# Two-layer graph network with neighbour quantiles: the kernel orders four queues by its own estimate of the engines

## The chip, the cores and the metric

The kernel runs on one core of one Trainium2 chip. The metric is the device time of one launch in microseconds (us); the time before is the median of three runs. The profile is one more execution, taken by the hardware profiler.

## The reference

There are 16 graphs of 1024 nodes with 64 features each (`x`: 16 x 1024 x 64, `adj`: 16 x 1024 x 1024 of zeros and ones, with self-loops). Two layers are computed, each followed by `layernorm(x + layer(x))`:

```python
# layer 0: thin out the neighbours, take quantiles, two dense layers
m = nb.sum(-1)                                   # neighbours without oneself
skip = where(m > 10, (m + 1) // 2, 1)
removed = nb & (skip > 1) & mask & ((rank + 1) % skip == 0)
valid = adj & ~(removed | removed.T)
sv = sort(where(valid, x[neighbour], big), over neighbours)   # for each node and feature
agg = sum over tau in (.25, .5, .75) of weight * interpolated sv[tau * (m - 1)]
y = relu((x + agg) @ W1 + b1) @ W2 + b2
# layer 1: messages of all neighbours
y = tanh(concat(x, adj @ x) @ W1 + b1) @ W2 + b2
```

The edge update of layer 1 doesn't reach the output and is left out.

## The kernel before

The work on a graph (a "batch" here) has three parts.

**Find** (`find`) loads the adjacency, turns it, ranks the neighbours on TensorE (`rank`), marks what is removed (VectorE, `removed`), adds up what stays (`stay`), and packs the neighbours of a node into words. The nodes of a batch are then sorted by their degree with a permutation matrix (`permutation`, `in_order`), and the numbers of each node's neighbours are drawn out with MAX8 and MATCH_REPLACE8, first from the words (`best_words`, `less_words`), then from codes made of them (`best_codes`, `less_codes`).

**Gather and sort.** 128 nodes of about equal degree are a tile; a batch has 8. Graphs go in groups: one batch, seven times two batches, one batch. `TILES` gives, for each tile of a group, the greatest and least count of cells. `gather` fetches, for the pair of tiles it is given, each neighbour's 64 features by one indirect DMA of GpSimd per cell (128 rows at a time; line L876), into one of a ring of four buffers g. `sort` then runs a sorting network over the cells: each step is one VectorE `tensor_tensor` min or max with two inputs, 64 to 1024 elements a partition. Only what the quantiles need is sorted. ScalarE multiplies the needed cells by their weights (L907), and TensorE adds them up (`add_up`, p_agg, L924 and L928). After that the ring's buffer is free.

**Close** (`close`) takes the sums back to node order (`back`, `return_to`), runs the dense layers, the norms, and layer 1, for which it loads the adjacency again and turns it in blocks.

The program is written as one stream. The comparisons of a pair of tiles go in a fixed merged order; find and close are lists of small steps (`Steps`), each with a weight in us, stretched over a time given beforehand, and a step is put between comparisons when its turn has come. "Time" is a counter `vector.now` in `Counted`, the wrapper through which all VectorE instructions are written (so they all stand at L443): it adds up the instructions' estimated durations. `Counted` also holds when GpSimd next wants to read its indices, `due`, every 1.32 us; if a comparison would come then, it writes first a `pause` (L437), a tiny one-input reduce of a cell written four comparisons ago. The framework then orders every engine's instructions itself, by its own model, within what the data allow.

Lists are made one group ahead while the present group is being gathered, and two ahead after that. A slot of the ring is given back a quarter into the next pair's comparisons. In the last group, `go_on_back` starts taking each pair back as soon as it is summed up.

Of the kernel before, what the change touches and what calls it, by code (L numbers as in the profile page):

```python
# [11 lines left out]
F32 = mybir.dt.float32  # L12
F16 = mybir.dt.float16
# [103 lines left out]
def network(n, least):  # L117
# [36 lines left out]
    return done, boxes(tuple((c, i) for i, c in enumerate(found))), found  # L154


@with_exitstack
def kernel(
# [236 lines left out]
    FINDING = 1.0  # L395
    CLOSING, CLOSING_LAST = 0.8, 60.0
    TURNING = 40.0
    RING = 4
    GATHER = 1.32
    pause = const.tile([P, 1], F32, name="pause")  # L400

# [6 lines left out]
    class Counted:  # L408

# [3 lines left out]
        def __init__(self):  # L413
            self.now = 0.0
            self.due = 0.0
            self.written = []

        def __getattr__(self, name):
            def size_of(x):
                n = 1  # L420
                for step, size in x.ap[1:]:
                    n *= size
                return n

            def issue(out, *args, **more):
                inputs = [a for a in args if isinstance(a, bass.AP)]
                n = max([size_of(out)] + [size_of(a) for a in inputs])
                each, more_us = 0.00104, 0.0
                if name in ("tensor_scalar", "tensor_copy"):
                    each = 0.00032 if out.dtype in (BF16, F16) and inputs[0].dtype in (BF16, F16) else 0.00053  # L430
                if name == "match_replace" or "accum_out" in more:
                    more_us = 0.07
                us = 0.067 + more_us + n * each
                two = name in ("tensor_tensor", "tensor_add", "tensor_sub", "tensor_mul",
                               "scalar_tensor_tensor")
                if two and self.now >= self.due and len(self.written) >= 4:
                    nc.vector.tensor_reduce(pause, self.written[-4], AX.X, ALU.max)  # L437
                    self.due = self.now + GATHER
                    self.now += 0.065
                elif not two and self.now + us >= self.due:  # L440
                    self.due = max(self.now, self.due) + GATHER
                self.now += us
# [3 lines left out]
    vector = Counted()  # L446

    class Steps:
# [3 lines left out]
        def __init__(self, within):  # L452
            self.steps, self.at, self.within = [], 0, within
            self.due = vector.now
# [13 lines left out]

        def go(self, all_of_it=False):
            scale = self.within / sum(us for us, _, _ in self.steps)  # L470
            while self.at < len(self.steps) and (all_of_it or self.due <= vector.now):
                us, what, args = self.steps[self.at]
                what(*args)
                self.at, self.due = self.at + 1, self.due + us * scale
# [5 lines left out]
    class Group:  # L480


        def __init__(self, number, start, G):
# [4 lines left out]
            self.pairs = [(k, k + 1) for k in range(0, NT * G, 2)]  # L488
# [6 lines left out]
    def find(group, i, within, pools):  # L495
# [7 lines left out]
        def begin():  # L503
            v["x_s"] = lists.tile([P, NT, C], F32, name="x_f", bufs=1)
            nc.sync.dma_start(v["x_s"], x[b].rearrange("(t p) c -> p t c", p=P))
            v["nb"] = mats.tile([P, NT, N], BF16, name="nb", tag="mat")
            v["a"] = [mats.tile([P, HT, N], F32, name="a", tag="mat") for _ in range(2)]
            for t in range(0, NT, 2):
                nc.sync.dma_start(v["a"][t // HT][:, t % HT:t % HT + 2],
                                  adj[b, t * P:(t + 2) * P, :].rearrange("(t p) k -> p t k", p=P))  # L510

        def adjacent(t):
# [3 lines left out]
            else:  # L516
                nc.scalar.activation(v["nb"][:, t], v["a"][t // HT][:, t % HT], AF.Sign)  # L517
# [8 lines left out]
        def features(i):  # L526
            if i == 0:
                v["part"] = lists.tile([P, NT, C], F32, name="part", bufs=1)
                nc.scalar.copy(part_of[0], v["x_s"])
            elif i == 1:  # L530
                vector.tensor_sub(v["part"], v["x_s"], part_of[0])
            elif i == 2:
                nc.scalar.copy(part_of[1], v["part"])
# [8 lines left out]
        def turn(j):  # L542
            p = ps.tile([P, NT, P], BF16, name="p_nb", tag="f")
            for t in range(NT):
                nc.tensor.transpose(p[:, t], v["nb"][:, t, block(j)], ident_h)  # L545
            if alone and j % 2:
                vector.tensor_scalar(v["nb_t"][:, j], p.rearrange("p t c -> p (t c)"), 0.0, None, op0=ALU.max)
            else:
                nc.scalar.activation(v["nb_t"][:, j], p.rearrange("p t c -> p (t c)"), AF.Relu)  # L549

        for k in range(4):
            to.add(1.5, features, k)
# [5 lines left out]
        def by_block(h):  # L558
# [4 lines left out]
            for j in range(NT):  # L563
                nc.tensor.matmul(v["p_cnt"][:NT, half], in_block[:, j], v["nb_t"][:, j, half],  # L564
                                 start=(j == 0), stop=(j == NT - 1), skip_group_check=True)
            nc.scalar.copy(v["blocks"][:, half], v["p_cnt"][:NT, half])
# [904 lines left out]
```

## Time and profile before

| what | value |
|---|---|
| median of three runs | 3017.12 us (3016.63 to 3021.24) |
| profiled execution | 3815.42 us, span 3813.7 us |
| mean granted TensorE clock, profiled | 0.709 |
| VectorE busy, profiled | 2329.5 us, 9225 instructions |
| GpSimd busy, profiled | 2104.7 us, 1943 instructions, 1859 of them gathers into g |
| first and last gather start | 103.7 us, 3683.2 us |

The profiled execution took 798 us more than the median of the runs. Its durations of single instructions can be used; its waits are those of that execution. In a row of the profile, `g<-in_x_dram,index` says what is written from what, `x1859 | 2075.7, 1117` is the count, the busy us and the mean ns of one, and behind it stands the time the engine was idle just before, and what ended most of it. All of VectorE's instructions stand at L443 (pauses at L437), so they are told apart by their tiles.

### The profile page before, as it was taken

What the parts mean: (1) busy time and instruction counts of PE and PEld (TensorE: products, weight loads), DVE (VectorE), ACT (ScalarE), POOL (GpSimd) and SP (SyncE); (2) the same over time, 40 slices, a digit from 0 to 9 for tenths busy, and PEclk for the clock granted to TensorE, in tenths of its full rate; (3) what the DMA queues carried; (4) which work ended last, traced back from release to release, by engine and by line L of the source; (5) the groups of instructions that cost most, each with busy time, mean ns of one, the idle gap of its engine ahead of it and who ended that gap; (6) DMA issues with size and microseconds to landing.
All of it is one profiled execution on the core that took longest, in us unless ns stands there. A gap on an engine that the chain in (4) does not pass through costs nothing.

```text
span 3813.7 us, 37663 instructions
## 1 busy us (share of the span) xinstructions
PE 1942.5 (51%) x10312; PEld 1070.0 (28%) x10312; DVE 2329.5 (61%) x9225; ACT 1324.3 (35%) x2945; POOL 2104.7 (55%) x1943
## 2 busy tenths in 40 slices
PE   5206523731565442963439635674336645674376
PEld 3103312420333221532224323332113323242133
DVE  4208624991598635885268844877248765768653
ACT  3204423431443332542325323544224334134123
POOL 1760346077654766167572677447571576757750
PEclk9556756765788666875669756786667866777578
DMA  2101111121212201222022212032021321242111
GB/s 99 20 19 48 58 50 32 65 52 24 64 44 87 66 18 62 82 66 43 17 67 93 67 30 65 23 105 64 18 66 28 94 58 26 60 117 62 20 47 29
DMA packets 268306, 205.67 MB, mean 54 GB/s; under 512 B 92634, under 2 KB 225290, under 8 KB 268086
## 3 DMA queue, kind: packets, MB, share of 16 engines
q1 hardware_dynamic: 207382, 147.10, 12.1%
q0 software_dynamic: 59744, 55.90, 7.5%
q8 instruction: 83, 1.36, 0.2%
q14 instruction: 137, 1.12, 0.1%
q10 hardware_dynamic: 960, 0.18, 0.0%
HBM read 203.97 MB, written 4.19 MB: 55 GB/s over the span
## 4 chain that ended last, share of the span: by engine, by line
PE 30%; another core or an unknown queue 25%; DVE 22%; ACT 9%; issue 8%; POOL 4%; DMA 1%; SPq 0%; ACTq 0%; DVEq 0%; POOLq 0%
DVE g L443 12%; PE p_msg L1144 5%; POOL g L876 4%; PE p_srt L687 3%; PE p_g L965 3%; PE p_adj L1135 2%; PE p_rank L596 2%; PE p_rank L593 2%; PE p_agg L924 2%; PE p_cnt L564 1%; PE p_nb L545 1%; ACT nb_t L549 1%; ACT g L907 1%; DVE codes L443 1%
## 5 line engine op out<-in xcount | busy, mean ns | idle before, releaser
L876 POOL DMA_INDIRECT g<-in_x_dram,index x1859 | 2075.7, 1117 | 1470.3 <-issue 560.1
L443 DVE TENSOR_TENSOR g<-g 128x128 f32<-128x128 f32 (+7 forms) x4982 | 1581.3, 373 | 199.7 <-remote 93.7
L545 PE MATMUL p_nb<-ident_h,nb 128*128 128x128 bf16 x1024 | 107.9, 280 | 649.6 <-DVE nb L443 261.9
L437 DVE TENSOR_REDUCE pause<-g 128x1 f32<-128x2 f32 x1021 | 148.5, 145 | 272.2 <-ACT g L907 240.5
L907 ACT ACTIVATE g<-g,weights 128x64 f32<-128x64 f32 x1006 | 260.0, 338 | 102.7 <-DVE g L443 84.3
L965 PE MATMUL p_g<-back,parts 128*64 128x512 bf16 x720 | 197.9, 425 | 186.6 <-DVE back L443 138.5
L443 DVE TENSOR_SCALAR gone<-gone,s 128x1024 bf16<-128x1024 f16 x128 | 64.3, 503 | 362.8 <-ACT gone L598 222.8
L598 ACT ACTIVATE gone<-p_rank,s 128x1024 f16<-128x1024 f32 x128 | 141.5, 1112 | 402.2 <-remote 303.2
L545 PEld LDWEIGHTS <-nb 128*128 128x128 bf16 x1024 | 92.6, 130 | 670.4 <-issue 489.9
L1144 PE MATMUL p_msg<-adj_t,x 128*64 128x512 f32 x416 | 232.3, 661 | 65.9 <-issue 30.4
L593 PE MATMUL p_rank<-after,blocks 8*128 8x512 bf16 x256 | 121.4, 474 | 282.0 <-ACT gone L598 147.5
L549 ACT ACTIVATE nb_t<-p_nb 128x1024 bf16<-128x1024 bf16 x124 | 122.1, 1023 | 375.0 <-remote 247.9
L924 PE MATMUL p_agg<-g,ident 128*128 128x128 f32 x918 | 161.6, 332 | 131.3 <-ACT g L907 83.7
L687 PE MATMUL p_srt<-pay,perm 128*128 128x323 bf16 x1024 | 187.0, 320 | 52.0 <-DVE x_q L443 29.4
L625 ACT ACTIVATE valid<-p_stay 128x1024 bf16<-128x1024 f32 x128 | 130.4, 1019 | 173.5 <-remote 95.0
L924 PEld LDWEIGHTS p_agg<-g,ident 128*128 128x128 f32 x918 | 143.0, 236 | 151.9 <-ACT g L907 96.4
L1137 ACT COPY adj_t<-p_adj 128x512 f32<-128x512 f32 x208 | 117.4, 584 | 162.6 <-PE p_adj L1135 79.0
L596 PEld LDWEIGHTS <-nb_t 128*128 128x128 bf16 x1024 | 70.6, 111 | 365.1 <-issue 365.1
L618 PE MATMUL p_stay<-nb,ident_h 128*128 128x512 bf16 x256 | 115.1, 450 | 105.8 <-ACT valid L625 56.3
L965 PEld LDWEIGHTS <-parts 128*64 128x64 bf16 x720 | 80.0, 119 | 280.1 <-issue 178.8
L517 ACT ACTIVATE nb<-a 128x1024 bf16<-128x1024 f32 x124 | 125.4, 1051 | 67.2 <-remote 27.1
L1135 PE MATMUL p_adj<-ident,a_block 128*128 128x128 f32 x832 | 138.6, 300 | 14.3 <-ACT z_t L1156 11.6
(188 smaller groups left out, 3054.9 us busy)
## 6 DMA issues: line engine op xcount, KB each, us to landing
a<-in_adj_dram SPq DMA_DIRECT2D x64, 1024.0 KB
a_block<-in_adj_dram SPq DMA_DIRECT2D x208, 256.0 KB
g<-in_x_dram,index POOLq DMA_INDIRECT x1859
a_ahead<-in_adj_dram SPq DMA_DIRECT2D x48, 256.0 KB
x_f<-in_x_dram SPq DMA_DIRECT2D x16, 256.0 KB
out_dram<-o SPq DMA_DIRECT2D x16, 256.0 KB
x_c<-in_x_dram SPq DMA_DIRECT2D x15, 256.0 KB
few<-index SPq DMA_DIRECT2D x45, 0.0 KB
```

The costliest lines, as they stand in the source:

```text
L437: nc.vector.tensor_reduce(pause, self.written[-4], AX.X, ALU.max)
L443: return getattr(nc.vector, name)(out, *args, **more)
L545: nc.tensor.transpose(p[:, t], v["nb"][:, t, block(j)], ident_h)
L549: nc.scalar.activation(v["nb_t"][:, j], p.rearrange("p t c -> p (t c)"), AF.Relu)
L593: nc.tensor.matmul(p[:, half_of(h)], v["blocks"][:, block(t)], after[:, half_of(h)], start=True, stop=False, skip_group_check=True)
L687: nc.tensor.matmul(p[:, k, :PAY], v["perm"][:, t, block(2 * at + k)], pay[:, t], start=(t == 0), stop=False, skip_group_check=True)
L876: nc.gpsimd.indirect_dma_start(out=part[:, j, :], out_offset=None, in_=x_rows, in_offset=bass.IndirectOffsetOnAxis(ap=group.index[:, v, sl ...
L907: nc.scalar.mul(g[:, cell], g[:, cell], group.weights[:, v, u, place:place + 1])
L924: nc.tensor.matmul(p, ident, it, start=(k == 0), stop=(k == most - 1), skip_group_check=True)
L965: nc.tensor.matmul(v["p_g"][h][:C, :HALF], v["parts"][:, k, q], m[:, half_of(h)], start=(k == 0 and v["start"]), stop=(k == 2 and q == v[" ...
L1135: nc.tensor.transpose(p[:, block(t)], m[:, t], ident)
L1144: nc.tensor.matmul(v["p_msg"][C:2 * C, :HALF], v["x1"][:, j, :], adj_t, start=(j == 0), stop=(j == NT - 1))
```

## The change

All `nc.tensor`, `nc.scalar`, `nc.sync` calls in the steps go through wrappers that estimate when an instruction can start and end. Inside the main loop, VectorE, TensorE, ScalarE and SyncE keep the order in which the program is written; GpSimd is left to the framework. The next comparison of a pair is picked among those whose inputs are ready, by how it fits GpSimd's next reading. When the reading is due, one of the one-input steps of find or close is put there if it is about due, else a pause, which now reads a constant. When an instruction's inputs are estimated to be late, comparisons are put in front of it. Tile k is paired with the tile k from the end. Lists are made up to two groups ahead at all times, and paced by when the gathers would run dry. Some rests and lags between steps are longer, and some buffers more.

```diff
+def order_of(n, least):            # which comparison must wait for which
...
-    FINDING = 1.0
-    CLOSING, CLOSING_LAST = 0.8, 60.0
+    IN_ORDER = {DVE, PE, Activation, SP}
+    FINDING_FIRST, FINDING = 95.0, 105.0
+    CLOSING, CLOSING_LAST = 110.0, 60.0
+    SPARE, EACH, EARLY, PACE, AHEAD, LATE = 10.0, 1.4, 3.0, (0.45, 1.2), 1.0, 2.0
+    ALONE = ("best_words", "less_words", "best_codes", "less_codes", "permutation", "removed", "back")
...
-    class Counted:
+    class Machine:                 # now, due, gathered; when each part of a tile was made and used
+        def ready(self, reads, writes):
+        def note(self, reads, writes, end):
...
+    class Engine:
+        def takes(self, name, out, reads):
+            n = max(size_of(a) for a in [out] + reads)
+            if self.kind == "ACT":
+                return 0.057 + 0.000845 * n, 0.12
+            if self.kind == "SP":
+                return 0.06, 2.0 + size_of(out) * out.ap[0][1] * 4e-6 / 0.2
+            if name == "transpose":
+                return (0.22 if reads[0].dtype == F32 else 0.107), 0.16
+            n = size_of(out)
+            return (max(0.43, 0.00168 * n) if reads[0].dtype == F32 else max(0.056, 0.00042 * n)), 0.16
...
+                if ready > machine.now + AHEAD:
+                    machine.fill(ready - AHEAD)
...
+    class Vector:
...
+                if ready > m.now:
+                    m.fill(ready)
+                    m.now = max(m.now, ready)
...
-                if two and self.now >= self.due and len(self.written) >= 4:
-                    nc.vector.tensor_reduce(pause, self.written[-4], AX.X, ALU.max)
+        def pause(self):
+            if machine.now >= machine.due:
+                nc.vector.tensor_reduce(pause, fill[:, :2], AX.X, ALU.max)
+                machine.due = machine.now + GATHER
+                machine.now += 0.065
...
     class Steps:
+        def pace(self):
+            left = sum(us for us, _, _ in self.steps[self.at:])
+            if self.until is None:
+                return self.within / sum(us for us, _, _ in self.steps)
+            return min(max((self.until() - machine.now) / max(left, 1.0), PACE[0]), PACE[1])
+        def alone(self, early):    # does the next step if it is one of ALONE and due within `early`
...
-            self.pairs = [(k, k + 1) for k in range(0, NT * G, 2)]
+            self.pairs = [(k, NT * G - 1 - k) for k in range(NT * G // 2)]
...
-        to.lagged(NT, (2.5, rank, 0), (0.1, removed, 3))
+        to.lagged(NT, (2.5, rank, 0), (0.1, removed, 5))
...
-                group.x_q[i] = lists.tile([P, NT, C], F32, name="x_q", bufs=4)
+                group.x_q[i] = lists.tile([P, NT, C], F32, name="x_q", bufs=6)
...
-                group.index = lists.tile([P, G, LIST], I32, name="index")
+                group.index = lists.tile([P, G, LIST], I32, name="index", bufs=3)
...
     def gather(group, at, sorts, lists):
...
             if start > filled[at % RING]:
-                least = 1
+                copy(part, none[:, :, None].to_broadcast([P, 2 * n, C]))
...
+            ready = machine.ready([group.index], [part])
+            machine.gathered = max(machine.gathered, machine.now, ready) + (many - 1) * EACH
+            landed.append(machine.gathered + 2.0)
...
-            for there, here, j in few(G):
-                nc.sync.dma_start(parts[0][here, j], got[there])
+            def give():
+                for there, here, j in few(G):
+                    nc.sync.dma_start(parts[0][here, j], got[there])
+            later.append((machine.gathered + 3.0, give))
...
+    def choose(tiles, latest):
+        gap = machine.due - machine.now
+        few, found = [], None
+        for t in tiles:
+            for n in t.ready[:5]:
+                wait = 0.05 if t is latest and t.last is not None and n in t.after[t.last] else 0.0
+                few.append((wait + 0.1 * (1 - t.left / t.all), t.us[n] + wait, t, n))
+        few.sort(key=lambda c: c[0])
+        if sum(us for _, us, _, _ in few) > gap > 0:
+            for some in range(1, 1 << len(few)):
+                these = [c for k, c in enumerate(few) if some >> k & 1]
+                over = sum(us for _, us, _, _ in these) - gap
+                if over >= 0:
+                    cost = over + sum(c[0] for c in these) / len(these)
+                    if found is None or cost < found[0]:
+                        found = cost, these[0]
+            return found[1][2:]
+        return few[0][2:]
...
+        def dry():
+            return machine.gathered + EACH * sum(TILES[g.G][k][0] - 1 for g, at in to_gather
+                                                 if g.number in found for k in g.pairs[at]) - SPARE
...
+            def turn(self):        # class Sorting
+                tiles = [t for t in self.tiles if t.ready and t.landed <= machine.now]
+                if not tiles:
+                    return False
+                if machine.now >= machine.due:
+                    if not any(steps.alone(EARLY) for steps in [f[2] for f in finding] + closing):
+                        vector.pause()
...
+                self.latest, n = choose(tiles, self.latest)
+                self.latest.issue(n)
...
-            ahead = 1 if to_gather and to_gather[0][0].number <= now else 2
-            if not finding and to_find and to_find[0][0].number <= now + ahead:
+            if not finding and to_find and to_find[0][0].number <= now + 2:
...
+                    steps.until = lambda group=group, i=i: min(begun + FINDING, dry() if i == group.G - 1
+                                                               else begun + (dry() - begun) / 2)
...
+        with tc.manual_schedule(engines=IN_ORDER):
+            for group in groups:
...
+                    sorting = Sorting(tiles, (group, at))
+                    machine.fill = sorting.fill
+                    while not sorting.done:
+                        around(group.number)
+                        if not sorting.turn():
+                            machine.now += 0.1
```

## The prediction

> **What bounds the kernel now.** I read the page's busy rows first, then the row of the gather, then who GpSimd (POOL) waited for, then the order of time in one quiet and one crowded stretch.
>
> ```profile
> PE 1942.5 (51%) x10312; PEld 1070.0 (28%) x10312; DVE 2329.5 (61%) x9225; ACT 1324.3 (35%) x2945; POOL 2104.7 (55%) x1943
> PE 30%; another core or an unknown queue 25%; DVE 22%; ACT 9%; issue 8%; POOL 4%; DMA 1%; SPq 0%; ACTq 0%; DVEq 0%; POOLq 0%
> L876 POOL DMA_INDIRECT g<-in_x_dram,index x1859 | 2075.7, 1117 | 1470.3 <-issue 560.1
> L443 DVE TENSOR_TENSOR g<-g 128x128 f32<-128x128 f32 (+7 forms) x4982 | 1581.3, 373 | 199.7 <-remote 93.7
> L437 DVE TENSOR_REDUCE pause<-g 128x1 f32<-128x2 f32 x1021 | 148.5, 145 | 272.2 <-ACT g L907 240.5
> ```
>
> No engine is full here, but the profiled execution (span 3813.7 us, 3815.42 us in all) is 798 us longer than the median of the three runs, 3017.12 us. A quarter of its chain is "another core or an unknown queue": mostly ScalarE waiting for a result of TensorE whose semaphore comes 10 to 27 us after the last matmul shown, while gathers run. All of PE, ACT and DVE stand still together for 634 us, and 509 us of that ends at such a late semaphore (added up from the trace). The runs without a profile have no room for it, so I take it as a thing of this execution and rebuild the runs' time from GpSimd's queue, which has to do 1867 gathers one by one.
>
> The quiet stretch and the crowded one (order of time; start, duration, engine, line):
>
> ```profile
> 158.56 0.99 POOL L876 DMA_INDIRECT g<-in_x_dram,index  x1 [0.30 <-issue]
> 159.86 0.99 POOL L876 DMA_INDIRECT g<-in_x_dram,index  x1 [0.30 <-issue]
> ...
> 3446.36 0.89 DVE L443 TENSOR_TENSOR g<-g 128x256 f32<-128x256 f32 x3
> 3446.42 1.23 POOL L876 DMA_INDIRECT g<-in_x_dram,index  x1 [0.30 <-issue]
> ...
> 3447.17 0.15 DVE L437 TENSOR_REDUCE pause<-g 128x1 f32<-128x2 f32 x1
> 3447.23 1.42 DVE L443 TENSOR_TENSOR g<-g 128x256 f32<-128x256 f32 x4
> 3447.95 1.58 POOL L876 DMA_INDIRECT g<-in_x_dram,index  x1 [0.30 <-issue]
> ...
> 3448.64 1.65 DVE L443 TENSOR_TENSOR g<-g 128x384 f32<-128x384 f32 x4
> 3449.83 1.01 POOL L876 DMA_INDIRECT g<-in_x_dram,index  x1 [0.30 <-issue]
> ```
>
> Alone, a gather starts every 1.30 us (0.99 + 0.30). Beside comparisons one takes 1.23 or 1.58 us and the next starts 1.53 and 1.88 us later. Over all 1842 successive pairs of gathers the step from start to start is 1.32 us where comparisons cover under 5% of it (771 pairs) and 1.56 us where they cover over 30% (911 pairs); its median is 1.41 us where they cover over 60%, so a tail makes the mean. Gathers delayed by over 0.3 us are 217 and hold 162 of the 226 us of delay.
>
> ```profile
> POOL g L876 <- PE p_agg L928: 331.4, 7, 101.1
> POOL g L876 <- ACT g L907: 156.9, 2, 156.6
> POOL g L876 <- PE p_agg L924: 126.2, 7, 33.7
> POOL g L876 <- DVE mid L443: 84.3, 1, 84.3
> ```
>
> These and smaller ones are the 900 us in which GpSimd had no gather to start: a list not made yet, or a ring slot not given back. So the profiled span is 103.7 (first gather) + 1842 x 1.44 = 2652 + 900 in gaps with some 27 of the gathers around them + 130 after the last gather.
>
> For the median run I keep everything but the gaps. With the same comparisons in less time, the crowded share rises from 911/1842 = 49% by 59/44 (the 1581 us of comparisons over about 2700 us, against over 3580) to 66%, so the mean step is 0.66 x 1.56 + 0.34 x 1.32 = 1.478 us. That gives 104 + 1867 x 1.478 = 2759 + 130 = 2993, and 24 us of gaps are left to make 3017. **The runs are bound by GpSimd's gathers, and mainly by what a comparison on VectorE costs each of them.**
>
> **The change, part by part.**
>
> *Comparisons by GpSimd's next reading* (`choose`, `pause`). Now two tiles' steps are merged by a fixed rule, and a step of up to 1.2 us can begin just before GpSimd wants to read. The change picks, among up to ten ready comparisons, those whose sum ends at the reading, so the overshoot falls from about half a step (mean 0.317 us) to near nothing. Bounds for a crowded gather: 1.32 us (never in the way) and 1.56 us (as now; worse is possible if the estimate drifts). I take 1.41, today's median in the crowded case: the tail is what a choice can take away. A thinner total raises the crowded share to 70%: 0.7 x 1.41 + 0.3 x 1.32 = 1.383, x 1867 = 2582, a gain of 177 us on 2759.
>
> *One-input steps in place of a pause* (`alone`). A pause is followed by the next comparison 0.06 us later, so 1021 cost about 65 us of VectorE, which is not the bound: 0 us. But of the 88 such steps of a batch (20 + 12 of words, 20 + 12 of codes, 8 each of permutation, removed, back), 24 are 16-bit `tensor_scalar` ones. Here a rule speaks against the change. Row: a gather that has such a permutation beside its reading steps 1.54 us in the median (15 of them), one with MAX8 on the words 1.30 us (19 of them). The Trainium skill, "SBUF — State Buffer", section "Who interferes with whom", says that `tensor_scalar` in a two-port mode holds the pair shared with GpSimd for the whole instruction and locks the other out, and that one-input work outside those modes doesn't. By the rule the 24 x 15 = 360 steps would cost their whole 0.48 us each, 173 us, and the gain would vanish; by the row 0.24 us, 86 us if all were put at a reading. Today's clock also counts them as openings, so I book nothing more and keep 86 us for the range.
>
> *Lists further ahead, their own paces, more buffers* (`now + 2` always, `dry`, `x_q` 6, `index` and `weights` 3). Worth at most the 24 us of gaps left. At the start of the second group the wait stays: 130 gathers last 180 us and two lists must be made in 2 x 95 us. I book 50 us of gaps against 24, since the order is now fixed. Lower bound 10, upper in the rival.
>
> *Pairs balanced.* Gathers and comparisons by pair (0.067 + 1.04 ns an element a step, the code's own rate, beside 0.283 us measured for 128 elements with overlap) go from 54 gathers with 50.1 us and 18 with 10.9 us to 42 with 38.7 us and about 28 with 18 to 22 us. The ring's slots come free evenly: inside the gaps. In the last group the last pair is (3, 4) instead of (6, 7), 18.9 us of comparisons for 12.9; most lies under its own gathers. The last tile alone is 9.3 for 6.2 us: +4 us on the tail, 134.
>
> *Order by hand on four queues.* It adds no instruction and no DMA. SP's small transfers into g (`few`) move behind an estimate, so that SP is not blocked by them; the summing after the last gather stays outside the hand order. What it costs is waiting at the head of a queue: at zero while VectorE has slack. VectorE is busy 2329.5 us, 52.7 of it before the first gather and 62.8 after the last, so 2214 us in a gather stretch of 2632: 418 us of slack, 28 us for each of the 15 later batches. That is the cover; the first rival takes it away.
>
> *Start.* Zeroing whole ring tiles on GpSimd is about 20,700 elements a partition at the trace's 0.98 us for 960, some 21 us from 11 us on, done before 104 us; SP, too, loads as before. 0 us.
>
> Sum: 104 + 2582 + 50 + 134 = **2870 us**, 147 below 3017 (4.9%).
>
> **The rivals.**
>
> *Slower: VectorE stands behind the list and close steps.* With a fixed order a `removed`, `x_q` or `d` that waits for TensorE holds every comparison behind it. For it: the estimate takes TensorE at full clock, while the page shows half and 0.709 in the mean; one `rank` runs 2.13 us on TensorE in the trace (126.69 to 128.82 us) against 0.88 in the estimate. VectorE's waits for such results (gone 362, s 102, x_q 93, d 82, low 39 us) are about 680 us now, 42 us a batch. 15 x 42 = 630 less 418 of slack is 212: 2870 + 212 = 3082 us. It decides from 28 us a batch, and 3017 is passed at 38. Against it: those waits are swollen by this execution's late semaphores, and `removed` now lags `rank` by five steps.
>
> *The step doesn't shrink.* The choice works blind: if VectorE or GpSimd runs off the estimate, comparisons still meet readings, and the 16-bit steps add theirs. Then 104 + 2759 + 134 + 10 = 3007 us, between 2985 and 3025: the change would not do what it says.
>
> *Better still.* Crowded gathers at 1.34 us, gaps 10: 104 + 1867 x 1.34 + 134 + 10 = 2750 us.
>
> **How the numbers follow.** About 0.2%, 6 us, is what a measurement can tell from no change. Chances: the forecast 0.52 (own range 2810 to 2940), better still 0.08, the step doesn't shrink 0.14 (0.09 of it faster, 0.03 the same, 0.02 slower), the slower rival 0.26 with one in a hundred of it the same. Faster 0.69, same 0.04, slower 0.27. The range runs from 2760, near the better case, to 3085, which takes in the slower rival's own figure; the worse half of that rival, about 0.13, and some 0.05 below stay out.
>
> **What would show it.** Right: gathers beside comparisons step 1.38 to 1.44 us and few exceed 1.3 us in duration; fewer `pause` rows than 1021 by several hundred; GpSimd's waits for `p_agg` and for list results shrink; still 1859 gathers. Wrong: VectorE's rows waiting for ACT or PE results grow past 28 us a batch with GpSimd waiting for `p_agg` (slots late) behind them; or gathers beside permutation, removed and back at 1.5 us and over, with the mean step unchanged. A first gather later than 110 us or a tail over 145 us would each take their difference off the gain. If TensorE's late semaphores stay in the profile, its span can go either way, and only the timed runs count.

## The result, and the profile after

The changed kernel takes **3038.93 us** (median of 4 runs, 3036.05 to 3041.53), the kernel before 3019.18 us (4 runs): a ratio of 1.0065, 95% interval 1.0048 to 1.0082. It is 0.65% slower, where 4.9% less was forecast. The profiled execution took 3041.53 us (span 3039.8, granted clock 0.766), so this profile can be read as the time itself. That of before could not, but times like its 3815 us are met without the profiler too: on three chips used below, timed runs of before took 3862, 3936 and 3902 us in the median, at a granted clock of about 0.70, and such runs ("late results" below) are compared only among themselves.

The page of the changed kernel, in the same rows as before: the busy line, the chain by engine, and the three groups.

```profile
PE 1904.4 (63%) x10326; PEld 1060.5 (35%) x10326; DVE 2403.2 (79%) x9330; ACT 1322.1 (43%) x2946; POOL 2084.7 (69%) x1951
PE 4%; DVE 3%; DMA 1%; ACT 1%; issue 0%; SPq 0%; DVEq 0%; ACTq 0%
L1042 POOL DMA_INDIRECT g<-in_x_dram,index x1859 | 2045.9, 1101 | 822.5 <-issue 525.5
L1088 DVE TENSOR_TENSOR g<-g 128x128 f32<-128x128 f32 (+6 forms) x4982 | 1588.3, 373 | 122.7 <-DMA g<-few_x 109.5
L579 DVE TENSOR_REDUCE pause<-fill 128x1 f32<-128x2 f32 x1125 | 163.5, 145 | 0.0
```

The chain says little here: it was followed back for 9% of the span only, so what bounds the kernel has to be read from queues. The same 1859 gathers are busy 30 us less than in the profile of before. VectorE has 1125 pauses for 1021, and it is busy for 79% of the span.

From the trace, start to start, 1854 gathers follow one another without a gap at 1.405 us in the mean: 1.435 where comparisons and other two-input work cover over 30% of the step (1312 of them, 71%), 1.312 where they cover under 5%. The span is then 114.9 (first gather) + 2605 + 189 (176 of gaps, and the 12 gathers beside them) + 131.0 (tail) = 3040 us. The waits of GpSimd that make up the gaps:

```profile
POOL g L1042 <- issue: 525.5, 1699, 8.1
POOL g L1042 <- DVE index L574: 106.8, 5, 66.5
...
POOL g L1042 <- DVE g L1088: 25.8, 8, 14.5
POOL g L1042 <- PE p_agg L539: 21.5, 3, 12.5
POOL g L1042 <- ACT g L539: 17.4, 5, 8.6
```

"issue" is mostly the 0.30 us between any two gathers. Of the 176 us of gaps, 107 are a list that isn't made yet (index: 66.5 us once, at 298 us, then 40 us in four waits at later group changes, the longest 16.0), and 69 are slots of the ring that come back late (p_agg and g, and one under "issue"; seven waits).

Who is late can be seen in VectorE's own waits. First the waits of the changed kernel's VectorE between first and last gather; the columns are us in total, times, and the longest:

```profile
DVE gone L574 <- ACT gone L539: 137.3, 63, 4.6
DVE g L1088 <- DMA g<-few_x: 109.5, 8, 22.4
DVE part L574 <- ACT pay L539: 39.7, 11, 19.9
DVE ln_st L574 <- ACT ln_st L539: 29.7, 17, 4.7
```

Added up, these and the smaller ones are 482 us of waits for results of ScalarE, TensorE and the small transfers. For a gather VectorE waits 2 us in the whole run. The table of windows (before, between, and behind the gathers; us, busy us and instructions of PE, PEld, DVE, ACT, POOL, then granted clock, DMA share and GB/s) has VectorE busy 2282 of 2794 us between them:

```profile
0.00:114.90 114.90, 57.44 (x369) 30.96 (x369) 60.85 (x230) 32.66 (x44) 30.76 (x85) 0.86 0.23 80
114.90:2908.80 2793.90, 1749.48 (x9576) 978.14 (x9577) 2282.30 (x8910) 1245.39 (x2814) 2052.48 (x1866) 0.76 0.26 68
2908.80:4500.00 1591.20, 97.50 (x384) 51.36 (x382) 60.04 (x193) 44.00 (x88) 1.51 (x1) 0.98 0.01 4
```

2282 + 482 = 2764 of 2794 us. That such a sum fills the stretch says little by itself, since an engine is nearly always busy or waiting; what tells is whom it waits for. **VectorE never gets ahead of the gathers any more, and the work that makes the lists and frees the slots passes through its queue.** The experiments show how much of the gaps this explains, and how much it doesn't. One group change (order of time on VectorE, then on GpSimd):

```profile
2021.74 0.67 DVE L574 TENSOR_REDUCE ln_st<-ln_sq 128x8 f32<-128x512 f32 x1
2027.08 0.20 DVE L574 RECIPROCAL ln_st<-ln_st 128x8 f32<-128x8 f32 x1 [4.67 <-ACT ln_st L539]
2027.20 0.51 DVE L574 TENSOR_REDUCE x_q<-p_srt 128x128 f32<-128x384 f32 x1
2027.62 0.68 DVE L574 TENSOR_TENSOR o<-d,ln_st 128x512 f32<-128x512 f32 x1
2028.22 0.55 DVE L574 TENSOR_REDUCE x_q<-p_srt 128x128 f32<-128x384 f32 x1
2032.55 0.56 DVE L574 TENSOR_REDUCE x_q<-p_srt 128x128 f32<-128x384 f32 x1 [3.78 <-ACT srt L539]
```
```profile
2038.62 1.00 POOL L1042 DMA_INDIRECT g<-in_x_dram,index  x1 [0.31 <-issue]
2055.62 0.99 POOL L1042 DMA_INDIRECT g<-in_x_dram,index  x1 [16.00 <-DVE index L574]
```

A close's `ln_st` waits 4.67 us for ScalarE at the head of the queue; the list's `x_q`, which stands behind it, starts by as much later, and a later `x_q` then waits itself. The plan wanted the list 10 us before the gathers ran out; it is there 16 us after. These two waits are 8.4 us of that; the rest had come together before.

### The profile page after: what moved, and what is told of

It reads as the page before. It is cut to its first block, busy times and chain, and to the rows that moved or that the text cites. A ratio compares the mean times of both kernels' runs of the same rounds, so it can differ in the third digit from the quotient of the medians.

```text
span 3039.8 us, 37578 instructions
## 1 busy us (share of the span) xinstructions
PE 1904.4 (63%) x10326; PEld 1060.5 (35%) x10326; DVE 2403.2 (79%) x9330; ACT 1322.1 (43%) x2946; POOL 2084.7 (69%) x1951
## 5 line engine op out<-in xcount | busy, mean ns | idle before, releaser
L1042 POOL DMA_INDIRECT g<-in_x_dram,index x1859 | 2045.9, 1101 | 822.5 <-issue 525.5
L1088 DVE TENSOR_TENSOR g<-g 128x128 f32<-128x128 f32 (+6 forms) x4982 | 1588.3, 373 | 122.7 <-DMA g<-few_x 109.5
L539 PE MATMUL p_agg<-g,ident 128*128 128x128 f32 (+1 forms) x1108 | 185.0, 338 | 162.7 <-ACT g L539 162.7
L539 PEld LDWEIGHTS p_agg<-g,ident 128*128 128x128 f32 x1108 | 177.2, 251 | 177.8 <-ACT g L539 153.2
L539 PE MATMUL p_nb<-ident_h,nb 128*128 128x128 bf16 x1024 | 93.2, 252 | 229.3 <-DVE nb L574 154.4
L539 PE MATMUL p_adj<-ident,a_block 128*128 128x128 f32 x832 | 152.9, 315 | 25.7 <-DMA a_block<-in_adj_dram 18.6
L539 PEld LDWEIGHTS <-nb 128*128 128x128 bf16 x1024 | 78.3, 115 | 254.9 <-issue 244.8
L579 DVE TENSOR_REDUCE pause<-fill 128x1 f32<-128x2 f32 x1125 | 163.5, 145 | 0.0
L539 PEld LDWEIGHTS p_adj<-ident,a_block 128*128 128x128 f32 x832 | 105.0, 160 | 148.7 <-issue 136.2
L539 PEld LDWEIGHTS <-perm 128*128 128x128 bf16 x1024 | 96.8, 103 | 106.4 <-DVE perm L574 31.3
```

Source lines behind the costliest of these rows:

```text
L539: return getattr(self.engine, name)(out, *args, **more)
L579: nc.vector.tensor_reduce(pause, fill[:, :2], AX.X, ALU.max)
L1042: nc.gpsimd.indirect_dma_start(out=part[:, j, :], out_offset=None, in_=x_rows, in_offset=bass.IndirectOffsetOnAxis(ap=group.index[:, v, sl ...
L1088: nc.vector.tensor_tensor(out, *ins, op=op)
```

## The experiments

Times are medians; each ratio is to before on the same chip, with its 95% interval. "Step", "gaps" and "tail" are worked out from each trace as above. For e1 to e4, for e5 to e12 (without e10) and for g15 before took 3018.66, 3017.83 and 3016.41 us: TensorE's results came in time.

| kernel | us | ratio | step us | gaps us | tail us |
|---|---|---|---|---|---|
| changed | 3038.93 | 1.0065 | 1.405 | 176 | 131.0 |
| e1: before, pause on a constant | 3076.66 | 1.0193 | 1.516 | 21 | 98.5 |
| e2: first lists in 60 us | 3044.15 | 1.0075 | 1.402 | 172 | 131.3 |
| e3: no order by hand | 3153.96 | 1.0444 | 1.506 | 103 | 107.0 |
| e4: no choice | 3036.05 | 1.0052 | 1.435 | 122 | 118.5 |
| e5: always a pause | 3020.93 | 0.9999 | 1.402 | 175 | 123.2 |
| e6: no 16-bit steps for a pause | 3018.68 | 1.0002 | 1.407 | 159 | 125.4 |
| e9: next batch's first steps early | 3029.06 | 1.0047 | 1.400 | 169 | 129.3 |
| e12: TensorE estimated slower | 3302.71 | 1.0954 | 1.393 | 469 | 115.5 |
| g15: five edits together | 3077.70 | 1.0204 | 1.407 | 224 | 115.2 |

**e1: the pause alone.** Before's pause reads a ring tile that was written a while ago, and so can wait for ScalarE; the changed one reads a constant, and so nothing in its data ties it to the comparisons.

```
-                    nc.vector.tensor_reduce(pause, self.written[-4], AX.X, ALU.max)
+                    nc.vector.tensor_reduce(pause, fill[:, :2], AX.X, ALU.max)
```

> The kernel before, with the pause reading a constant instead of a cell written four comparisons ago. Theory A: the 240 us in which pauses waited for ScalarE belong to that one profiled execution; the time stays within 10 us of 3019. Rival B: pauses do wait behind the weight multiplies in every run, and the constant takes 40 to 100 us away. Besides, this is a second profile of the old order of work: if TensorE's late semaphores are not part of every execution, its span is near 3020 us and shows the real split of the time: by the prediction a mean step of 1.48 us and 24 us of gaps; by the rival reading (the old step was already about 1.41) some 100 to 200 us of gaps.

Measured: 1.0193 (1.0163 to 1.0224), 58 us slower, which neither theory gave. The trace shows why the pauses no longer work. The framework orders VectorE's queue here, and a pause that reads a constant may go anywhere. Three stretches of its trace; the second column of numbers is the length, then the pauses' busy us and their number:

```profile
0.00:115.00 115.00, 49.28 (x321) 0.89 0.23 82
115.00:1250.00 1135.00, 7.47 (x48) 0.74 0.24 65
1250.00:3062.00 1812.00, 92.47 (x652) 0.77 0.26 68
```

321 of the 1021 pauses stand before the first gather, and from 162 to 1250 us there is none; cut at the same places, before's profile has 0, 280 and 713, and the changed kernel 3, 413 and 710. Without pauses comparisons run in unbroken trains, and a gather can stand for as long as one lasts:

```profile
199.31 13.77 POOL L876 DMA_INDIRECT g<-in_x_dram,index  x1 [0.30 <-issue]
199.59 12.62 DVE L443 TENSOR_TENSOR g<-g 128x576 f32<-128x576 f32 x36
```

In e1 35 gathers take over 3 us, 157 us together; in before's profile 12 do, 43 us, and in the changed kernel 2, 6 us. The mean step in e1 is 1.54 us from 200 to 1200 us and 1.49 from 1300 to 2900, where the pauses are back. So e1 prices pauses that have left their place, and not the operand where the pause stays. It is also the nearest thing to a trace of before's order with TensorE's results in time. VectorE's waits between the gathers there:

```profile
DVE g L443 <- DMA g<-in_x_dram,index: 433.9, 19, 46.5
DVE gone L443 <- ACT gone L598: 55.1, 67, 2.6
DVE x_q L443 <- ACT srt L691: 38.1, 32, 4.5
```

VectorE waits 434 us for gathers and only 210 us for others, and GpSimd has 21 us of gaps: here GpSimd is the bound, at 1.516 us a gather (1.623 beside comparisons). Against e1 the changed kernel wins 1867 x 0.111 = 207 us in steps and loses 155 in gaps and 32 in the tail. Before itself has no trace with results in time; if all of e1's 58 us lie in the step, before's is 1.485 us (an estimate), and the changed kernel wins some 150 us in steps against it.

**e2 and e9: the 66 us at the start of the second group.** e2 plans the first lists over 60 us, e9 takes the first steps of the next list into the one before.

```
-    FINDING_FIRST, FINDING = 95.0, 105.0
+    FINDING_FIRST, FINDING = 60.0, 105.0
```

> The changed kernel with FINDING_FIRST 60 instead of 95, so the lists of the second group are written more closely after the first. Theory A (GpSimd's 66 us gap at 297 us is a list that comes late because it is paced late): the gap falls to 20 us or less, the time by 40 to 65 us to 2975 to 3000. Rival B (list steps and comparisons share VectorE, so what is won at 297 us comes back as later gaps or longer steps): 3025 to 3040.

```
+                if group.number <= 1 and to_find and to_find[0][0].number <= 1:
+                    nxt = find(*to_find[0], FINDING_FIRST, pools)
+                    at = [what.__name__ for _, what, _ in steps.steps].index("list_of_words")
+                    steps.steps[at:at] = nxt.steps[:1 + NT]
```

> The changed kernel where the loads and the sign step (begin, adjacent) of the next batch stand in the order before the words of the present batch are drawn out, for the first three batches. Theory A (the 66 us gap at 297 us comes from the fixed order: ScalarE stands 30 us at hats while the next adjacency has long landed): the gap falls to 10 to 35 us and the time by 30 to 55 us, to 2985 to 3010. Rival B (VectorE is the bound, a gap closed early opens later): 3030 to 3045.

Measured: the gap is 70.7 us with e2 and 63.1 with e9, for 66.5. Neither the planned pace nor the late start of the next list makes it; that theory fell. The list of batch 2 is ready at 365 us, at 328 in e1, while the first group's gathers now end at 298 us instead of 318. Why that list is 37 us later stays open. The order by hand is not needed for it: e3, below, has a gap of 65.7 us at the same place.

**e3 and e4: which part shortens the step.** e3 gives all queues back to the framework and keeps the rest; e4 keeps the order by hand and takes the first of the ready comparisons instead of the picked ones.

```
-        with tc.manual_schedule(engines=IN_ORDER):
+        if True:
```

> The changed kernel, same program text, but the framework orders all queues again. Theory A (the fixed order costs: VectorE stands at the head of its queue for few_x, removed, d and the lists): 20 to 100 us faster than the change, 2940 to 3020. Rival B (the picked order is what shortens the gathers' step and is lost when the framework reorders): the step goes from 1.407 back to 1.45 to 1.50, 80 to 170 us slower, 3120 to 3210.

```
-        if sum(us for _, us, _, _ in few) > gap > 0:
+        if False:
```

> The changed kernel without the choice by GpSimd's next reading: always the first of the ready comparisons in the order of waits and progress. Theory A (the choice shortened the step): crowded gathers go from 1.44 to about 1.50 us, mean 1.407 to 1.45, 60 to 100 us slower, 3100 to 3140. Rival B (the pause at the due time does the work, the choice adds little): mean step within 0.01 of 1.407, time within 20 us of 3039.

Measured: 1.0444 (1.0397 to 1.0491) and 1.0052 (1.0037 to 1.0068). Without the order by hand the step is 1.506 us in the mean, but e3 loses more than the picked order. Its pauses, too, read the constant and leave their places: 320 of 1125 stand before the first gather, and from 458 to 1659 us there is none. Where it has none (600 to 1600 us) it steps 1.56 us. From 1600 to 2900 us, where all three kernels have their pauses, e3 steps 1.449 us, e4 1.439 and the changed kernel 1.401. There the choice is worth 0.04 us a gather, and the order by hand without the choice (e4) is only 0.01 ahead of no order by hand (e3). What the order by hand does besides is to keep the pauses in place.

Over the whole run the choice shortens the step by 0.030 us, 1867 x 0.030 = 56 us, and brings no time: gaps grow by 54 us and the tail by 12 where it is used. This is the run that shows that gathers are no longer the bound. In e4, as in the changed kernel, VectorE hardly waits for a gather (8 us); in e3, as in e1, it does (284 us).

e3 also shows what VectorE's full queue doesn't explain. All its 103 us of gaps are lists that come late, about as much as the 107 us in the changed kernel, though VectorE has time to wait for gathers. Late slots, 69 us in the changed kernel, it has none. With e3's slower gathers this is no clean test, but late lists may go with how they are planned, and late slots with the order by hand or the faster gathers. Which of these it is isn't shown.

**e5 and e6: steps in place of a pause.** e5 always pauses; e6 lets no `permutation`, `removed` or `back` stand for a pause, but words and codes.

```
-                    if not any(steps.alone(EARLY) for steps in [f[2] for f in finding] + closing):
-                        vector.pause()
+                    vector.pause()
```

> The changed kernel with a pause at every due reading: no one-input step of find or close takes its place. Theory A (the gathers' step is set by real openings; a permutation or other 16-bit step is none): mean step 1.39 to 1.40 instead of 1.405, some 300 more pauses, whose 0.065 us each cost VectorE 20 us; time within 15 us of 3039. Rival B (list steps get their speed from being pulled forward by this): lists later, gaps over 250 instead of 176 us, time 3070 to 3120.

```
-    ALONE = ("best_words", "less_words", "best_codes", "less_codes", "permutation", "removed", "back")
+    ALONE = ("best_words", "less_words", "best_codes", "less_codes")
```

> The changed kernel where only MAX8 and MATCH_REPLACE8 steps may take a pause's place, not permutation, removed and back (16-bit tensor_scalar). Theory A (these three hold the port: gathers beside permutation step 1.50 us in the median, beside MAX8 1.30): mean step 1.405 to about 1.39, 20 to 40 us faster if nothing else changes. Rival B (the time is held by VectorE, so what the gathers win comes back as gaps): within 10 us of 3039.

Measured: 0.9999 (0.9984 to 1.0015) and 1.0002 (0.9989 to 1.0015), about 18 and 20 us under the changed kernel, and level with before. Both have 1149 pauses for the changed kernel's 1125, where some 300 more were expected: in the net, steps took a pause's place at some two dozen readings only. Words and codes for a pause cost nothing that can be told; the three others carry the cost. But it isn't in the step, which stays (1.402 and 1.407): the tail shrinks by 8 and 6 us, the gaps by 1 and 17, and VectorE's waits for `few_x` fall from 109.5 to 71 us. With so few places touched, these runs don't test the 173 us that the prediction worked out for all 360 of the 16-bit steps. The delay that it read from its rows is there again: in e1's trace 18 gathers with `permutation` beside them, and hardly any comparison, step 1.54 us in the median, those with MAX8 1.30.

**e12: a slower TensorE in the estimate.** The prediction's slower rival held that the estimate takes TensorE as too fast. Here its time for a bf16 matmul is doubled.

```
-            ... else max(0.056, 0.00042 * n)), 0.16
+            ... else max(0.11, 0.00088 * n)), 0.16
```

> The changed kernel with the estimate of 16-bit matmuls at the measured rate (0.88 ns a column, at least 0.11 us) instead of half of it. Theory A (VectorE stands behind removed and others because the estimate has TensorE too fast: 148 us for gone, 72 for d): gone's waits fall under 60 us, gaps by 50 us or more, time 2960 to 3010. Rival B (those waits lie in VectorE's slack): time within 15 us of 3039, gaps about 176 us.

Measured: 1.0954 (1.0936 to 1.0973), 264 us more than the changed kernel. VectorE's waits for `gone` fell to 40 us as that theory had it, but the gaps grew to 469 us and the theory that too fast an estimate makes them fell: GpSimd now waits 257 us in 4 stretches behind `p_msg` and 62 in one behind `p_adj`, both of the closes. That the slower estimate placed steps of list and close later is the likely reason, and was not followed up.

**The edits against the gaps.** `few` planned to land 24 us after the gathers instead of 8 (e10); SPARE 30 instead of 10, so that lists end earlier (e13, f13); these two with e6 and e9 (e14, f14); and the same with closes over 85 us instead of 110 (e15, f15, g15). e16 is the changed kernel itself.

```
-            landed = [max(t, machine.gathered + 8.0) for t in landed]
+            landed = [max(t, machine.gathered + 24.0) for t in landed]
-    CLOSING, CLOSING_LAST = 110.0, 60.0
+    CLOSING, CLOSING_LAST = 85.0, 45.0
-    SPARE = 10.0
+    SPARE = 30.0
```

> The changed kernel with one number altered: the small transfers into the ring (few) are taken to land 24 us after GpSimd's gathers instead of 8, so the comparisons on them stand later in VectorE's order. In the changed kernel VectorE waited 109.5 us for them in 8 waits. Theory A (what the hand order puts too early stands at the head of VectorE's queue, and the gaps of GpSimd come from VectorE running behind its estimate): these waits fall below 30 us, the gaps at the group changes (8 to 16 us each, 110 us together without the first) shrink by about half, and the time falls by 30 to 80 us to 2960 to 3010. Theory B (VectorE has slack for these waits, the gaps have another cause): the waits fall, the gaps stay, and the time is within 10 us of the changed kernel's, 3029 to 3049.

> The changed kernel with SPARE 30 instead of 10: a group's lists are planned to end 30 us before GpSimd's gathers run out by the estimate, instead of 10. Theory A (the lists come late only because the plan leaves them 10 us and the real queue lags by about as much as the gaps show): the gaps after 300 us, some 110 us, fall below 50 us, and the time falls by 40 to 80 us to 2960 to 3000. Theory B (VectorE has no room: lists that come earlier push the comparisons and the closes back): gaps shrink, but the mean step, the slots (GpSimd waiting for p_agg) or the tail take it back, and the time is 3020 to 3050.

> The changed kernel with four edits together: no 16-bit or one-input steps of permutation, removed and back in place of a pause (e6), the next batch's first steps taken into the list before (e9), SPARE 30 and few landing after 24 us. Theory A (each removes its own part of the gaps): 20 us from the first, 10 from the second, 40 from SPARE, 30 from few: about 2940 us, at most 2980. Theory B (what one wins another term takes back, since VectorE is the fuller of the two queues): 3000 to 3025, no better than the best of its parts.

> The same four edits, and the closes planned over 85 us instead of 110 (45 instead of 60 for those not paced). In the changed kernel the last closes but two end 9 us after the last gather, where before's order with another pause had them 24 us ahead of it, and the tail was 131 instead of 98.5 us. Theory A (the tail is longer because closes run late): the tail falls to about 105 us and the time is 20 to 30 us under that of the four edits alone. Theory B (closes that are packed closer take VectorE from the comparisons in the gather stretch): the tail falls but gaps or steps grow by as much, and the two kernels are within 10 us.

These four met a chip with late results: before took 3862.17 us, and they 1.087 (1.0734 to 1.1006), 1.1028 (1.0909 to 1.1147), 1.0982 (1.0878 to 1.1087) and 1.0879 (1.0757 to 1.1001) times that. So the changed kernel itself was run beside the edits.

> The changed kernel once more, unaltered, beside the kernel before on the same chip. The four runs just made stand on a chip where TensorE's results come late, as in the profile of before (before took 3862 us there instead of 3018), and the changed kernel itself has not run there. If the chip is such a one again: theory A (a fixed order on four queues passes every late result on to all that stands behind it) gives a changed kernel 7 to 12% slower than before; theory B (the four edits did that) gives 0 to 2% slower. If the chip is one where the results come in time: 3030 to 3050 us, 0.3 to 1.0% slower than before, as measured.

> SPARE 30 instead of 10 once more, to have it beside the changed kernel on one chip. Theory A (the plan leaves the lists too little time): 40 to 80 us under the changed kernel of this call. Theory B (what lists win, steps, slots or the tail take back): within 15 us of it.

> The four edits once more (no permutation, removed and back steps for a pause; early first steps of the next batch; SPARE 30; few landing after 24 us), beside the changed kernel on one chip. Theory A (the parts add up): 60 to 100 us under the changed kernel of this call. Theory B (what one wins another gives back): 10 to 25 us under it.

> The four edits and closes over 85 us once more. Theory A (the longer tail comes from closes that run late): tail near 105 us and 20 to 30 us under the four edits alone. Theory B: within 10 us of them.

Another chip of the same condition: before 3936.32 us, the changed kernel 1.1014 (1.0937 to 1.1092), the edits 1.0985, 1.0932 and 1.0828 (1.0755 to 1.0901). With SPARE alone it is 6 us under the changed kernel, with four edits 41, with the shorter closes 62. The first expectation of e16 is the one that came: **with late results the changed kernel is 10% slower than before, and with the edits 8 to 10%.** The reason given with it, that the fixed order passes lateness on, fits the waits of GpSimd in e16's trace, which has 1441 us of gaps:

```profile
POOL g L1042 <- PE p_agg L539: 473.6, 12, 68.4
POOL g L1042 <- DVE index L574: 418.9, 5, 226.9
POOL g L1042 <- ACT g L539: 251.3, 19, 47.2
```

The step is even shorter than in time, 1.372 us. In the profile of before, itself of this condition, the gaps are 916 us, and `p_agg` and `g` on ScalarE hold the ring up for 615 us where here it is 725; lists, 419 us in five waits here, are among what grew most. That e16's VectorE waits 1726 us between the gathers and before's 1328 agrees. That it is the order by hand and no other part wasn't run in this condition.

> The four edits and closes over 85 us, a third time, for a chip where TensorE's results come in time (before near 3018 us there). Both runs so far had before at 3862 and 3936 us. There the five edits together were 1.4% faster than the changed kernel. Theory A (gaps and tail come from lists, few and closes planned too late): gaps fall from 176 to under 80 us, the tail from 131 to about 105 us, and the time is 2930 to 2980 us, 1 to 3% under before. Theory B (what one wins, another gives back, VectorE being the fuller queue): 2995 to 3020 us, level with before.

On a chip with results in time the five edits take 3077.70 us, 1.0204 (1.0175 to 1.0233): slower than the changed kernel by 39 us, where with late results they were 1.4% faster than it (4260.06 for 4322.26). Neither expectation gave that, but the second named the way: what one wins, another gives back. The tail fell to 115 us, the waits for `few_x` to 25, list waits after the first to 1 us. In their place stand three waits of 32 to 36 us, one a group. GpSimd, and below it TensorE, at the first of them:

```profile
1521.40 1.00 POOL L1042 DMA_INDIRECT g<-in_x_dram,index  x1 [0.30 <-issue]
1554.30 1.27 POOL L1042 DMA_INDIRECT g<-in_x_dram,index  x1 [31.91 <-PE p_nb L539]
```
```profile
1526.70 13.05 PE L539 MATMUL p_g<-back,parts 128*64 128x512 bf16 x48 [40.53 <-DVE back L574]
...
1545.44 0.62 PE L539 MATMUL p_nb<-ident_h,nb 128*128 128x128 bf16 x8
1547.52 1.12 PE L539 MATMUL p_h<-g_t,w1a_s 64*128 64x512 f32 x2 [1.46 <-ACT g_t L539]
1548.57 4.96 PE L539 MATMUL p_agg<-g,ident 128*128 128x128 f32 x28
```

The page names `p_nb` as what released the gather, but the work that gives back a slot is `p_agg`, which ends at 1553.5 us, just before it. It stood in TensorE's queue behind the close's `p_g`, which waited 40.53 us for VectorE's `back`. The list comes in time, and the slot is late instead.

**e17: VectorE's order alone.**

```
-    IN_ORDER = {mybir.EngineType.DVE, mybir.EngineType.PE, mybir.EngineType.Activation, mybir.EngineType.SP}
+    IN_ORDER = {mybir.EngineType.DVE}
```

> The changed kernel with only VectorE's queue in the order of its own planner; TensorE's, ScalarE's and SyncE's are ordered by the framework again. Theory A (the short step needs VectorE's order alone, and the gaps come from the other three fixed queues, where p_agg and the list's matmuls stand behind steps that wait): the mean step stays at 1.40 us, the gaps fall from 176 to under 110, and the time is 2940 to 3000 us, under before. Theory B (VectorE is the fuller queue and lags its plan by itself; the gaps are its own): step 1.40, gaps 150 to 250, 3010 to 3060 us. Theory C (the framework's orders, made with another clock than VectorE's, make VectorE wait at its head): VectorE's waits and the gaps grow, over 3080 us, and the order by hand is needed on all four.

It met late results: before 3901.96 us, ratio 1.1199 (1.1114 to 1.1285), where the changed kernel had 1.1014 on another such chip. Freeing three queues doesn't help there: gaps are 1517 us, and VectorE waits 1781 us between the gathers. In the usual condition this was not run, so which of the four queues makes the late slots stays open. Nor were the balanced pairs and the lists further ahead tried by themselves.

## Why the prediction was wrong, point by point

The sum was 104 + 2582 + 50 + 134 = 2870; measured is 115 + 2618 + 176 + 131 = 3040 (2618 are all gathers, those beside gaps too). The terms miss by 11, 36, 126 and -3 us.

- **What bounds it now** was right in its main line. The 798 us of late results were left out of the sum, and the runs to be compared indeed had none; e1's 21 us of gaps fit the 24 that it worked out. But "a thing of this execution" was wrong: timed runs can meet it, and there the change costs 10%.
- **The step** was nearly right: 1.435 us beside comparisons for 1.41, a crowded share of 71% for 70%, a mean of 1.405 for 1.383. Giving the gain to the choice holds where pauses are in place (0.04 of 0.05 us, e3 and e4). What the prediction missed is that the pauses, once they read a constant, stay in place only by the order by hand; without it the step is 1.506.
- **One-input steps**: booked 0, with 86 us in the range; e5 and e6 show 18 to 20. The fewer pauses did not come, 1125 for 1021. The pause's new operand was not priced at all; e1 shows 58 us for it where no order by hand holds the pause in place.
- **Order by hand, "at zero while VectorE has slack"** is the step that failed. The cover was 418 us: 2632 of gathers less 2214 busy, with no waits of VectorE in it. In e1, whose gathers are slower, there was such room, 434 us of VectorE waiting for gathers. In the changed kernel VectorE is busy 2282 us, 68 more, and waits 482 us for others, 64 more than the cover; with 30 left over that is the 162 us by which the gather stretch (2794 us) exceeds the forecast's 2632. This splits the time and doesn't prove a cause; e4 does the proving, where 56 us of slower gathers cost nothing. What the order, with the faster gathers, cost is seen as 69 us of slots that come late, booked at nothing; e3 has none.
- **Lists, 50 us of gaps**: all gaps are 176, and 107 of them are lists. At the start of the second group the wait was named, and sized at too little: 66.5 us by itself. Since e3 has 103 us of late lists without the order by hand, VectorE's full queue alone doesn't explain this term; what does stays open.
- **Pairs and start**: the tail came as booked, 131 for 134, but by luck: the 130 it started from belong to the profile with late results, and e1 has 98.5. Against e1 the closes of batches 14 and 15 run later (they end 88 and 125 us after the last gather, 48 and 93 there). The first gather came at 115 instead of 104 us; in the other traces with results in time it lies between 113 and 127.

**The slower rival came**, at a smaller price than it was given. It was to decide from 28 us of VectorE's waits a batch, with late slots behind them; the waits are 482/15 = 32 (403/15 = 27 in e3, without the order by hand), and the late slots are there. Its 42 us a batch were taken from a profile with late results, which made the rival 3082 us. With 32 it gives 2870 + 64 = 2934, still under before; only the 68 us of added busy time, which it did not have, and 30 of rest bring 3032. The prediction knew this mechanism and gave it a chance of 0.26: it discounted the waits, since only a profile with late results showed their size.

## What to carry to other kernels

When the fullest queue is made faster, redo the balance of the next one with its waits in it: busy time alone left VectorE 418 us here, and its waits for others came to 482. Ask of a trace whom each engine waits for: 434 us for its partner in one trace here and 2 us in the next means that it no longer has room. Tuning of dates then moves a wait from one place to another, as the five edits did.

An instruction that is put in for its place has to be tied to that place, by what it reads or by a fixed order. The pause was tied by its old operand; with a constant it drifted away from the gathers wherever the framework ordered the queue.

A kernel whose order is fixed by an estimate should be timed in the worst condition its runs meet: this one is 0.65% slower with results in time, 10% with late ones.

## What the runs showed of the hardware

Executions of one program can differ, in a way that the profile names only as "another core or an unknown queue". On three chips before took 3862 to 3936 us in the median, on the others 3016 to 3019, with a granted clock of about 0.70 or 0.76. In e16 TensorE, VectorE and ScalarE all stand still for about 840 us, in the same kernel with results in time for about 50. What makes the results late isn't shown, nor how much of it the lower clock is, nor whether it stays with a chip.

A gather of GpSimd that starts beside an unbroken train of two-input comparisons can stand until the train ends: 13.77 us in e1, where the usual one takes 1.0. With a one-input `tensor_reduce` of two elements, 145 ns long, put between comparisons, the longest gather of the changed kernel takes 3.30 us.
